# One core, a conditioned recurrent block with an MLP: the first stage put in a set order, with the stores of 1/rms, the sums of weights and the squares moved

## The chip, the cores and the metric

The kernel runs on one core of one Trainium2 chip. The metric is the device time of one execution in microseconds (us). Lower is better. TensorE (PE in the profile) does the matrix products; its weight loads have a row of their own (PEld). VectorE is DVE, ScalarE is ACT, GpSimd is POOL, and SyncE (SP) issues most of the DMAs.

## The reference

For B = 2 sequences of L = 2048 tokens with D = 512 channels, everything in float32:

```python
# _L0_cond_ref: a linear layer whose weight is scaled per sequence
styles = w @ (affine_w * gain).T + affine_b
ws = weight[None, :, :] * styles[:, None, :]
dcoefs = jax.lax.rsqrt(jnp.sum(ws * ws, axis=2) + 1e-08)
xm = x * styles[:, None, :]
y = jnp.einsum('blc,oc->blo', xm, weight)
y = jnp.clip(y * dcoefs[:, None, :] + bias, -CLAMP, CLAMP)

# _L0_attn_ref: a gated linear recurrence, then a gated MLP
h = _rms_norm(hidden_states, norm_w)
gate = jax.nn.gelu(h @ fc_gate_w.T + fc_gate_b, approximate=False)
hs = h @ fc_w.T + fc_b
r = jax.nn.sigmoid(h @ fc_r_w.T + fc_r_b)
i = jax.nn.sigmoid(h @ fc_i_w.T + fc_i_b)
a = jnp.exp(-8.0 * jax.nn.softplus(alpha) * r)
s = jnp.sqrt(1.0 - a * a) * hs * i          # o_t = a_t * o_(t-1) + s_t
hs2 = out * gate + residual
h2 = _rms_norm(hs2, norm2_w)
g2 = jax.nn.gelu(h2 @ mlp_gate_w.T + mlp_gate_b, approximate=False)
f2 = h2 @ mlp_fc_w.T + mlp_fc_b
return f2 * g2 @ out_w.T + out_b + hs2
```

Behind it stands a third part (several layer norms, a combining MLP and an int8 product), which the change doesn't touch.

## The kernel before

**Tiling.** The tokens are cut into NS = 4 blocks of S = 1024, two per sequence, with channels in the partitions. Every large product is a **unit**: the function `paired` computes a product of 2 x 2 blocks with seven products instead of eight, by sums of weights and sums of operands. A unit has seven steps. Each step multiplies one slot of the weight tile (slots 0 to 6; slots 4, 5, 2 and 6 hold the sums and differences) with one operand, for u = 0 and u = 1, four instructions each. Step 1 goes to the bank pair "a", whose values ScalarE copies out with the function `tap` (k1); steps 3 and 5 go on adding in the same banks and are copied again (k2, k3). Step 2 fills bank pair "b" and steps 4 and 7 pair "d". A product that adds to a bank must wait until the copy of the bank is taken. The argument `at` holds extra work: the functions under (n, u) are written right behind the half u of step n.

**Stages.** `cond(s)`, s = 0 to 3, is the first stage, one unit for each block (here: pass s). `recur(s, last)` is the recurrence, four units for each block. `up` is the first half of the MLP, six units for each block. `down` and what comes later are not touched.

**The start.** DMAs on SP bring `cols` (small vectors), `affT` (512 KB), `condT` (the first stage's weight, 1 MB) and `x` of the first block (2 MB). TensorE makes the styles (L326), then the sums of squares for dcoef: four row products into four groups of 32 columns (`rows_of`, L310), a copy on ScalarE (L311), and four transposing products (`columns_of`, L319). VectorE scales the weight by the styles (`style(0)`, L360) and makes its sums (L365 to L368), and makes the operand sums (`operand_sums`, L251 to L254). The first product of pass 0 comes behind all products of dcoef.

**1/rms.** `squares` adds up squares of the four outputs of a pass. `inv_rms` returns four functions: `total` (products with ones, L420), `log` and `exp` on ScalarE (L428, L432), and `step` on VectorE (L437 to L439) with four stores of 1 KB to `r_d` on SP's queue (L441). `then`, in the next pass or in the second unit of `up`, writes all four at once behind step 3. `normed_halves` loads a block again (L449), loads 1/rms broadcast to all partitions (L451), and multiplies the two in four chunks on VectorE (L454).

**Weights.** `load_rec(o, behind)` loads the weight of unit o of the recurrence in four DMAs and lets GpSimd make its sums (`combine`, L121 to L124). A copy of 1 x 8 values from `behind` into the tile (L537) keeps the DMAs from starting earlier than `behind` is written. `load_up(p)` does the same for the MLP, without such a copy. `load_rec(s, ...)` is called behind pass s with an operand sum of that pass as `behind`.

**The recurrence's rest.** `links` returns what is left of a unit after its products, and the next unit carries it out: `decay` and `rest_of_decay`, `scan` (VectorE, step 3), `gated` (step 4, which writes yr, L584 to L587), `square` of yr on ScalarE (L593, behind the first half of step 5) and `total`, an addition on VectorE (L597, behind step 5).

**Order.** A scheduler orders the instructions of every engine by priorities and by a simulated time. Inside `with ordered()` the engines TensorE, VectorE and ScalarE keep the order in which the program is written. Before, that holds for pass 3 and for the recurrence with the first unit of `up`. SP and GpSimd are always left to the scheduler.

Of the kernel before, what the change touches and what calls it, by code (L numbers as in the profile page):

```python
# [9 lines left out]
FP = mybir.dt.float32  # L10
BF = mybir.dt.bfloat16
AF = mybir.ActivationFunctionType
ALU = mybir.AluOpType
# [4 lines left out]
P = 128  # L18
# [32 lines left out]
def adaln_attn_ffn(ctx: ExitStack, tc: tile.TileContext, a: dict, out: bass.AP):  # L51
# [221 lines left out]
    def load_x(s):  # L273
# [3 lines left out]
        return t  # L277

    affT = row("affT").rearrange("p (j o) -> p j o", j=2)
# [3 lines left out]
    load_w(condT, a["condT"])  # L283
    x_first = load_x(0)
# [4 lines left out]
    nc.vector.tensor_copy(identb, ident)  # L289
    ones = const.tile([P, P], FP, name="ones")  # L290
    nc.vector.memset(ones, 1.0)
    one = ones[:, 0:1]
    epsc = const.tile([P, 1], FP, name="epsc")
    nc.vector.memset(epsc, 1e-6)

    groups = ident.rearrange("p (j r) -> p j r", r=G)
    summing = const.tile([P, G], FP, name="sums")
    nc.vector.tensor_reduce(summing, groups.rearrange("p j r -> p r j"), AX.X, ALU.add)  # L300
    apart = const.tile([P, 3, B], FP, name="apart")
    nc.vector.tensor_copy(apart, groups[:, 0:3, 0:B])
    nc.vector.tensor_add(apart[:, 0, :], groups[:, 0, 0:B], groups[:, 3, 0:B])

# [17 lines left out]

    ps = mm("ps_styles")
    for o in range(C):
        for j in range(2):
            nc.tensor.matmul(  # L326
                ps[:, o * B : o * B + B], affT[:, j, ts(o, P)], col("cond_512", j * B, B),
                start=(j == 0), stop=(j == 1),
            )
    for o in range(C):  # L330
        nc.vector.tensor_scalar(
            styles[:, o, :], ps[:, o * B : o * B + B], 1.0 / 16.0, col("L0_cond_affine_b", o),
            ALU.mult, ALU.add,
        )
# [3 lines left out]
    nc.vector.tensor_mul(st2[:, :, 0:B], styles, styles)  # L338
    wsq = []
    for c in range(C):  # L340
        t = tp.tile([P, T], FP, tag="k", name=f"wsq_{c}")
        nc.scalar.activation(t, condT[:, c, :], AF.Square)
        wsq.append(t)
    rows_k = tp.tile([P, T], FP, tag="k", name="ps_dcoef_k")
    rows_of("ps_dcoef", [(st2[:, c, :], wsq[c]) for c in range(C)], rows_k)
    ps = columns_of("ps_dcoef", rows_k, summing[:, 0:B])
    dflat = dcoef.rearrange("p c b -> p (c b)")
    dv = small.tile([P, 2, C * B], FP, name="dv")
    nc.vector.tensor_scalar(
        dv[:, 0, :], ps.rearrange("p c b -> p (c b)"), 1e-8, None, ALU.add  # L350
    )
    nc.scalar.activation(dflat, dv[:, 0, :], AF.Sqrt)
    nc.vector.reciprocal(dflat, dflat)
    refine(dflat, dv[:, 0, :], dv[:, 1, :])


    def style(b):
        w = w_cond[b]
        for c in range(C):
# [5 lines left out]
        nc.vector.tensor_add(w[:, 4], w[:, 2], w[:, 3])  # L365
        nc.vector.tensor_sub(w[:, 5], w[:, 4], w[:, 0])
        nc.vector.tensor_sub(w[:, 2], w[:, 0], w[:, 2])
        nc.vector.tensor_sub(w[:, 6], w[:, 1], w[:, 5])  # L368

    style(0)  # L370

# [4 lines left out]
    e_, u_, l_, d_, m_ = (sa[:, k, :] for k in range(5))  # L376
    nc.vector.tensor_scalar(m_, al, -1.0, None, ALU.mult)
    nc.vector.tensor_tensor(e_, al, m_, ALU.min)
    nc.scalar.activation(e_, e_, AF.Exp)
    nc.vector.tensor_scalar(u_, e_, 1.0, None, ALU.add)  # L380
    nc.scalar.activation(l_, u_, AF.Ln)
    nc.vector.tensor_scalar(d_, u_, -1.0, None, ALU.add)
    nc.vector.tensor_sub(d_, e_, d_)
    nc.vector.reciprocal(u_, u_)
    nc.vector.tensor_mul(d_, d_, u_)
    nc.vector.tensor_add(l_, l_, d_)
    nc.vector.tensor_scalar(m_, al, 0.0, None, ALU.max)
    nc.vector.tensor_add(l_, l_, m_)
    nc.vector.tensor_scalar(kal, l_, -8.0, None, ALU.mult)


    aw = col("aw", 0, 6)
    smx = small.tile([P, 2], FP, name="smx")
    nc.vector.reduce_max(smx[:, 0:1], aw, AX.X)
    nc.vector.tensor_scalar(wsm, aw, smx[:, 0:1], None, ALU.subtract)
    nc.scalar.activation(wsm, wsm, AF.Exp)
    nc.vector.reduce_sum(smx[:, 1:2], wsm, AX.X)
    nc.vector.reciprocal(smx[:, 1:2], smx[:, 1:2])
    nc.vector.tensor_scalar(wsm, wsm, smx[:, 1:2], None, ALU.mult)

# [8 lines left out]
    def inv_rms(tot, m, s):  # L409
# [25 lines left out]
        def step():  # L435
            r, q = held["r"], held["q"]
            nc.vector.scalar_tensor_tensor(q, held["ps"], D * 1e-6, q, ALU.add, ALU.mult)  # L437
            nc.vector.tensor_scalar(q, q, -0.5 / D, 1.5, ALU.mult, ALU.add)
            nc.vector.tensor_mul(r, r, q)  # L439
            for j in range(4):  # L440
                nc.sync.dma_start(r_d[m, s][:, ts(j, n)], r[32 * j : 32 * j + 1])  # L441

        return total, log, exp, step

# [16 lines left out]

    def then():
        while rest:
            for f in rest.pop(0):
                f()

# [9 lines left out]
    def cond(s):  # L476
        b = s // PER_S
        xs = operands(x_first if s == 0 else load_x(s), f"xT_{s}")
        y = {}

# [5 lines left out]
        def tap(u, ps, n):  # L486
            o = u if n < 3 else u + 2
            t = tp.tile([P, T], FP, tag="k", name=f"k{n}")
            nc.scalar.activation(
                t, ps, AF.Identity, scale=dcoef[:, o, b : b + 1], bias=col("L0_cond_bias", o)  # L490
            )
            return t
# [20 lines left out]

        at = {(3, 1): [then]}
        if s == NS - 1:

            Bt, chunks = rec_norm(0)
            ahead[:] = operand_sums(Bt, "hT_0")
            at[2, 1] = chunks[0:2]
            at[4, 1] = chunks[2:4]  # L520
            at[6, 1] = ahead[1][0:1]
        paired([w_cond[b]], xs, f"y_{s}", tap, put(0, a_), put(0, b_), out21, put(2, b_), at)
# [5 lines left out]
        rest.append(inv_rms(tot, 1, s))  # L528
        return xs

# [18 lines left out]
    chain = {}  # L549

    def merged(*ds):
        got = {}
        for d in ds:
            for k, fs in d.items():
                got.setdefault(k, []).extend(fs)
        return got

    def links(s, o, r, i, f, g, last, new, tots):
# [36 lines left out]
        def total():  # L595
# [8 lines left out]
            (1, 0): [decay], (1, 1): [rest_of_decay], (3, 1): [scan], (4, 1): [gated],  # L604
            (5, 0): [square], (5, 1): [total],
        }

    def recur(s, last):
        new = small.tile([P, C], FP, tag="carry", name=f"carry_{s}")
        tots = []  # L610
        for o in range(C):
# [27 lines left out]
            elif o == 1 and rest:  # L639
                total, log, exp, step = rest.pop(0)  # L640
                at = merged(at, {(3, 1): [total], (4, 1): [log], (5, 1): [exp], (6, 1): [step]})
            elif o >= 2:
                if o == 2:
                    Bt, chunks = rec_norm(s + 1) if s + 1 < NS else up_norm(0)
                    at = merged(at, {(2, 1): chunks[0:1], (6, 1): chunks[1:3]})
                else:
                    ahead[:] = operand_sums(Bt, f"hT_{s + 1}")
                    at = merged(at, {(2, 1): chunks[3:4], (6, 1): ahead[1][0:1]})
# [7 lines left out]

    def load_up(p):
        w = weight(f"w_up_{p}", {1: "A", 2: "B", 5: "C"}.get(p))
        for u in range(2):
            for k, n in ((0, "w_mg"), (2, "w_mf")):  # L660
# [9 lines left out]
    def up(s, xs, parts, at):  # L670
        for p in parts:
# [26 lines left out]
            def out22(u, ps, kept):  # L698
# [5 lines left out]
                [w_up[p]], xs, f"up_{s}_{p}", keep, out1(a_), out1(b_), out21, out22,  # L704
                at if p == 0 else {(3, 1): [then]} if p == 1 else {},
            )

    w_dn = []
# [9 lines left out]

    def ordered():
        return tc.manual_schedule(  # L720
            engines={mybir.EngineType.PE, mybir.EngineType.DVE, mybir.EngineType.Activation}
        )
# [898 lines left out]
```

## Time and profile before

| what | us |
|---|---|
| median of 3 runs (lowest, highest) | 2043.91 (2043.42, 2048.09) |
| the profiled execution | 2045.46 |
| its span, first to last instruction | 2043.7 |
| mean granted TensorE clock in it | 0.996 |
| first product of pass 0 (y_a) starts | 15.16 |
| first product of the recurrence (rec_a) starts | 120.75 |
| first product of the MLP (up_a) starts | 509.94 |

How much each engine works in the stages that the change edits, by the view of windows (us from the span's start; columns: length, then busy time and count of TensorE, its weight loads, VectorE, ScalarE and GpSimd, then TensorE's granted clock, the busy share of the DMA engines, and GB/s):

```profile
80.00:100.00 20.00, 19.34 (x46) 8.22 (x44) 18.74 (x18) 9.72 (x12) 14.04 (x8) 1.00 0.79 270
100.00:150.00 50.00, 45.62 (x109) 19.84 (x110) 31.31 (x33) 22.62 (x29) 12.19 (x9) 0.97 0.44 155
...
120.00:144.00 24.00, 24.00 (x58) 10.61 (x57) 11.76 (x13) 8.42 (x12) 5.93 (x4) 1.00 0.57 201
144.00:168.00 24.00, 24.00 (x64) 10.39 (x63) 12.67 (x15) 20.22 (x24) 0.00 (x0) 1.00 0.23 65
168.00:192.00 24.00, 24.00 (x58) 10.61 (x57) 16.93 (x17) 17.21 (x20) 0.00 (x0) 1.00 0.15 45
...
528.00:552.00 24.00, 21.37 (x53) 8.89 (x52) 9.98 (x13) 8.91 (x13) 0.00 (x0) 0.93 0.16 66
```

A stretch in which TensorE's busy time equals its length has no wait of TensorE in it. The granted clock is a mean over the stretch.

### The profile page before, as it was taken

Reading aid. Unit: us, or ns where it says so; the run is one execution under the profiler, and the core shown is the slowest. Engines: PE = TensorE matmul, PEld = TensorE weight load, DVE = VectorE, ACT = ScalarE, POOL = GpSimd, SP = SyncE. Lnnn points to the kernel's source line nnn. Section 1 sums busy time; section 2 is a strip of 40 time slices with the busy share of each in tenths; the row PEclk is TensorE's granted clock in tenths of the full one; section 3 lists DMA queues with packets and bytes.
Section 4 is the critical chain, followed back from the end, with each engine's and each line's share of the span. In section 5 each row is a group of like instructions: output and inputs, shape, how many; then the busy total and the mean of one; then the engine's idle time right before and its main releaser. Section 6 shows DMA issues by size and latency. Waiting matters only on the chain.

```text
span 2043.7 us, 17016 instructions
## 1 busy us (share of the span) xinstructions
PE 2016.0 (99%) x6374; PEld 1067.9 (52%) x6374; DVE 1195.5 (58%) x1798; ACT 653.2 (32%) x861; POOL 157.9 (8%) x126
## 2 busy tenths in 40 slices
PE   8999999999999999999999999999999999999997
PEld 4444444444444444444444444434877777777774
DVE  6766666667533324234325475476588678678675
ACT  4547777776422222222221000001302302302301
POOL 1420000012100000000010000072000000000000
PEclk9999999999999999999999999999999999999999
DMA  6731213232212212111335766624111111111000
GB/s 214 260 136 52 83 52 95 60 113 82 93 42 76 78 41 93 41 42 52 102 116 179 225 223 216 220 94 165 41 43 62 60 45 62 61 43 62 21 21 21
DMA packets 83971, 193.54 MB, mean 95 GB/s; under 512 B 6544, under 2 KB 34742, under 8 KB 79792
## 3 DMA queue, kind: packets, MB, share of 16 engines
q1 hardware_dynamic: 79280, 175.67, 25.3%
q0 software_dynamic: 4608, 16.78, 2.5%
q8 instruction: 50, 0.82, 0.2%
q14 instruction: 33, 0.27, 0.0%
HBM read 133.27 MB, written 58.75 MB: 94 GB/s over the span
## 4 chain that ended last, share of the span: by engine, by line
PE 93%; DVE 4%; DMA 1%; issue 1%; ACT 0%; SPq 0%; DVEq 0%; ACTq 0%
PE up_a L132 16%; PE ps_h_a L132 11%; PE rec_a L132 10%; PE up_d L132 8%; PE dn_a L132 7%; PE ps_h_d L132 6%; PE rec_d L132 5%; PE ps_o L1397 5%; PE up_b L132 4%; PE dn_d L132 4%; PE ps_h_b L132 3%; PE rec_b L132 3%; PE y_a L132 2%; PE dn_b L132 2%; PE ps_f L1421 1%; PE y_d L132 1%
## 5 line engine op out<-in xcount | busy, mean ns | idle before, releaser
L132 PE MATMUL up_a<-h,w_up 128*128 128x512 f32 x384 | 172.6, 592 | 0.0
L132 PE MATMUL dn_a<-op,w_dn 128*128 128x512 f32 x384 | 167.4, 594 | 0.0
L699 DVE SCALAR_TENSOR_TENSOR prod<-up_d,cols,k 128x512 f32<-128x512 f32 x48 | 36.0, 751 | 200.7 <-ACT k L265 200.7
L265 ACT COPY k<-up_a 128x512 f32<-128x512 f32 x144 | 84.2, 585 | 195.4 <-PE up_a L132 195.4
L679 ACT ACTIVATE gate<-gate,cols 128x512 f32<-128x512 f32 x96 | 68.8, 721 | 218.3 <-DVE gate L678 218.3
L132 PE MATMUL up_a<-h2T,w_up 128*128 128x512 f32 x288 | 129.5, 592 | 0.0
L132 PEld LDWEIGHTS up_a<-h,w_up 128*128 128x128 f32 x384 | 72.9, 190 | 91.9 <-issue 89.7
L132 PEld LDWEIGHTS dn_a<-op,w_dn 128*128 128x128 f32 x384 | 72.2, 190 | 88.8 <-issue 86.5
L132 PE MATMUL rec_a<-hT,w_rec 128*128 128x512 f32 x256 | 115.6, 593 | 1.1 <-ACT k L265 1.1
L132 PE MATMUL rec_a<-h,w_rec 128*128 128x512 f32 x256 | 115.1, 592 | 0.0
L1397 PE MATMUL ps_o<-int_w,h 128*128 128x512 f32 x224 | 103.6, 605 | 0.0
L132 PEld LDWEIGHTS up_a<-h2T,w_up 128*128 128x128 f32 x288 | 54.7, 190 | 68.9 <-issue 68.9
L132 PE MATMUL up_d<-h,w_up 128*128 128x512 f32 x192 | 87.5, 599 | 0.0
L132 PE MATMUL up_b<-h,w_up 128*128 128x512 f32 x192 | 86.3, 592 | 0.0
L132 PE MATMUL dn_d<-op,w_dn 128*128 128x512 f32 x192 | 84.2, 595 | 0.0
L132 PEld LDWEIGHTS rec_a<-hT,w_rec 128*128 128x128 f32 x256 | 48.5, 190 | 63.0 <-issue 60.3
L132 PEld LDWEIGHTS rec_a<-h,w_rec 128*128 128x128 f32 x256 | 48.6, 190 | 61.2 <-issue 61.2
L265 ACT COPY k<-rec_a 128x512 f32<-128x512 f32 x96 | 55.7, 580 | 70.2 <-PE rec_a L132 70.0
L678 DVE TENSOR_TENSOR gate<-up_b,k 128x512 f32<-128x512 f32 x48 | 32.9, 690 | 76.1 <-PE up_b L132 74.7
L132 PE MATMUL up_d<-h2T,w_up 128*128 128x512 f32 x144 | 65.2, 592 | 0.0
L1397 PEld LDWEIGHTS ps_o<-int_w,h 128*128 128x128 f32 x224 | 40.2, 189 | 46.5 <-issue 46.5
L132 PE MATMUL ps_h_a<-tT,w_int 128*128 128x256 f32 x256 | 64.2, 385 | 0.0
(389 smaller groups left out, 3475.4 us busy)
## 6 DMA issues: line engine op xcount, KB each, us to landing
pp_d<-prod SPq DMA_DIRECT2D x48, 512.0 KB
op<-pp_d SPq DMA_DIRECT2D x16, 1536.0 KB
x<-in_xT SPq DMA_DIRECT2D x4, 2048.0 KB
y_d<-y SPq DMA_DIRECT2D x16, 512.0 KB
h<-y_d SPq DMA_DIRECT2D x4, 2048.0 KB
yr<-y_d SPq DMA_DIRECT2D x16, 512.0 KB
hs_d<-yr SPq DMA_DIRECT2D x16, 512.0 KB
h<-hs_d SPq DMA_DIRECT2D x4, 2048.0 KB
```

What stands on the lines that cost most here:

```text
L132: ins = nc.tensor.matmul(ps, ws[k // 2][:, slot, k % 2, ts(u, P)], xs[k], start=(first and k == 0), stop=(last and k == n - 1), skip_group ...
L265: nc.scalar.copy(t, ps)
L678: nc.vector.tensor_add(gate[u][:, half], ps, kept)
L679: nc.scalar.activation(gate[u][:, half], gate[u][:, half], AF.Gelu, bias=col("L0_attn_mlp_gate_b", fs[u]),)
L699: nc.vector.scalar_tensor_tensor(prod[u][:, b_], ps, col("L0_attn_mlp_fc_b", fs[u]), kept, ALU.add, ALU.add)
L1397: nc.tensor.matmul(ps, h1[:, c, ts(j, P)], w2[:, c, :], start=(c == 0), stop=(c == C - 1))
L1421: nc.tensor.matmul(ps, qT[:, ts(c, P)], rq[:, c, :], start=(c == 0), stop=(c == C - 1))
```

## The change

1. **Pass 0 in a set order.** `with ordered()` now holds for passes 0 and 3. The preparations become functions that are called at chosen places: the constants, the styles, the scaling and the sums of the weight (`style` returns eight functions), the small work on alpha and aw (`alpha_1` to `alpha_4`), and the weight of the second sequence (`style(1)`) spread over steps 4 to 7. `condT` is loaded in two halves and the first x in four quarters. The rows of dcoef come between the two halves of step 1, its columns behind step 1, and the copies k1 are written behind them.
2. **Idle products.** `busy(n)` writes n products of ones with ones, 128 x 128, into a bank that nobody reads: 9 before the styles and 10 behind them.
3. **1/rms.** The four stores become a fifth function, `store`, on ScalarE's queue. `then` is gone: the five functions are spread over steps 4 to 7 of the next pass, and over steps 3 to 7 of a unit in the recurrence and in `up`.
4. **Pass 3.** The four chunks of the norm go behind steps 2 (two), 3 (one) and the first half of 5 (one), instead of two behind step 2 and two behind step 4.
5. **Weights.** `load_rec` is called for units 0, 1, none, and 2 and 3 behind the passes 0 to 3, and `behind` is the last output of the pass (y[1]). `load_up` has a `behind` too: the same output of pass 3 for w_up 0 to 2, and the last gate of the first unit of `up` for w_up 3 to 5.
6. **Squares of yr.** `square` moves from the first half of step 5 to behind step 6, `total` from behind step 5 to the first half of step 7.

```diff
+    for h in (0, 1):
+        nc.sync.dma_start(condT[:, 2 * h : 2 * h + 2, :], by_chunks(a["condT"])[:, 2 * h : 2 * h + 2, :])
+    x_first = halves("x_0")
+    for h, half in ((0, a_), (1, a_), (0, b_), (1, b_)):
+        of = slice(2 * h, 2 * h + 2)
+        nc.sync.dma_start(x_first[:, of, half], by_chunks(a["xT"][0])[:, of, half])
...
+    idle = mm("idle")
+    def busy(n):
+        for _ in range(n):
+            nc.tensor.matmul(idle[:, 0:P], ones, ones, start=True, stop=True)
...
+        def store():
+            r = held["r"]
             for j in range(4):
-                nc.sync.dma_start(r_d[m, s][:, ts(j, n)], r[32 * j : 32 * j + 1])
-        return total, log, exp, step
+                nc.scalar.dma_start(r_d[m, s][:, ts(j, n)], r[32 * j : 32 * j + 1])
+        return total, log, exp, step, store
...
-    def then():
-        while rest:
-            for f in rest.pop(0):
-                f()
+    def parts_of_rest(*keys):
+        if not rest:
+            return {}
+        return {k: [f] for k, f in zip(keys, rest.pop(0))}
+    AT = ((3, 1), (4, 1), (5, 1), (6, 1), (7, 1))
...
     def cond(s):
         b = s // PER_S
-        xs = operands(x_first if s == 0 else load_x(s), f"xT_{s}")
-        y = {}
+        at = parts_of_rest((4, 0), *AT[1:])
+        if s == 0:
+            busy(9)
+            constants()
+            styles_of()
+            busy(10)
+            parts = style(0)
+            for f in parts[0:2]:
+                f()
+            nc.vector.tensor_mul(st2[:, :, 0:B], styles, styles)
+            wsq = squares_of_weight()
+            for f in parts[2:6]:
+                f()
+            xs, sums = operand_sums(x_first, "xT_0")
+            sums[0]()
+            sums[1]()
+            other = style(1)
+            at = {
+                (2, 1): [sums[2], parts[7], sums[3], alpha_1], (3, 1): [alpha_2],
+                (4, 1): [alpha_3] + other[0:2], (5, 1): [alpha_4] + other[2:4],
+                (6, 1): other[4:6], (7, 1): other[6:8],
+            }
+        else:
+            xs = operands(load_x(s), f"xT_{s}")
+        y, late = {}, []
...
-            nc.scalar.activation(
+            late.append(lambda: nc.scalar.activation(
                 t, ps, AF.Identity, scale=dcoef[:, o, b : b + 1], bias=col("L0_cond_bias", o)
-            )
+            ))
+            if s == 0 and n == 1:
+                if u == 0:
+                    late.insert(0, dcoef_rows(wsq))
+                    return t
+                dcoef_columns(late.pop(0))
+                parts[6]()
+            while late:
+                late.pop(0)()
             return t
...
-        at = {(3, 1): [then]}
...
-            at[2, 1] = chunks[0:2]
-            at[4, 1] = chunks[2:4]
-            at[6, 1] = ahead[1][0:1]
+            at = merged(
+                at, {(2, 1): chunks[0:2], (3, 1): chunks[2:3], (5, 0): chunks[3:4], (6, 1): ahead[1][0:1]}
+            )
...
-            (5, 0): [square], (5, 1): [total],
+            (6, 1): [square], (7, 0): [total],
...
-                at = merged(at, {(3, 1): [total], (4, 1): [log], (5, 1): [exp], (6, 1): [step]})
+                at = merged(at, parts_of_rest(*AT))
...
+        nc.vector.tensor_copy(w[0:1, 0:4, 0, 0:2 * P:P], behind)
...
-                at if p == 0 else {(3, 1): [then]} if p == 1 else {},
+                at if p == 0 else parts_of_rest(*AT) if p == 1 else {},
...
-        with ordered() if s == NS - 1 else nullcontext():
-            xs = cond(s)
-        if s == 0:
-            style(1)
-        load_rec(s, xs(5)[0][0:1, 0:8].rearrange("p (a b) -> p a b", b=2))
+        with ordered() if s in (0, NS - 1) else nullcontext():
+            done = cond(s)
+        for o in ((0,), (1,), (), (2, 3))[s]:
+            load_rec(o, done)
     for p in range(3):
-        load_up(p)
+        load_up(p, done)
...
-        up(0, xs, (0,), merged(chain, {(2, 1): sums[2:4]}))
+        done = up(0, xs, (0,), merged(chain, {(2, 1): sums[2:4]}))
     for p in range(3, FC // 2):
-        load_up(p)
+        load_up(p, done)
```

More of the change, by code (lines that the diff above doesn't have):

```diff
@@ L277, in load_x, with ordered @@
         return t
+    def ordered():
+        return tc.manual_schedule(
+            engines={mybir.EngineType.PE, mybir.EngineType.DVE, mybir.EngineType.Activation}
+        )
     affT = row("affT").rearrange("p (j o) -> p j o", j=2)
@@ L282, in adaln_attn_ffn @@
     condT = part(weight("condT"), C, D)
-    load_w(condT, a["condT"])
-    x_first = load_x(0)
+    for h in (0, 1):
[4 more added lines that the diff above has]
+        nc.sync.dma_start(x_first[:, of, half], by_chunks(a["xT"][0])[:, of, half])
+    ones = const.tile([P, P], FP, name="ones")
+    nc.vector.memset(ones, 1.0)
+    one = ones[:, 0:1]
     ident = const.tile([P, P], FP, name="ident")
@@ L288, in adaln_attn_ffn, with constants @@
     identb = const.tile([P, P], BF, name="identb")
[L289 to L292, printed above, removed]
     epsc = const.tile([P, 1], FP, name="epsc")
-    nc.vector.memset(epsc, 1e-6)
-    groups = ident.rearrange("p (j r) -> p j r", r=G)
     summing = const.tile([P, G], FP, name="sums")
-    nc.vector.tensor_reduce(summing, groups.rearrange("p j r -> p r j"), AX.X, ALU.add)
     apart = const.tile([P, 3, B], FP, name="apart")
-    nc.vector.tensor_copy(apart, groups[:, 0:3, 0:B])
-    nc.vector.tensor_add(apart[:, 0, :], groups[:, 0, 0:B], groups[:, 3, 0:B])
+    def constants():
+        groups = ident.rearrange("p (j r) -> p j r", r=G)
+        nc.vector.memset(epsc, 1e-6)
+        nc.vector.tensor_copy(identb, ident)
+        nc.vector.tensor_reduce(summing, groups.rearrange("p j r -> p r j"), AX.X, ALU.add)
+        nc.vector.tensor_copy(apart, groups[:, 0:3, 0:B])
+        nc.vector.tensor_add(apart[:, 0, :], groups[:, 0, 0:B], groups[:, 3, 0:B])
     def rows_of(name, parts, t):
@@ L320, in columns_of @@
         return ps
[L323 to L328, printed above, removed]
-            )
[L330 to L333, printed above, removed]
-        )
+    idle = mm("idle")
@@ new lines, in busy, with styles_of @@
+    def busy(n):
+        for _ in range(n):
+            nc.tensor.matmul(idle[:, 0:P], ones, ones, start=True, stop=True)
+    def styles_of():
+        ps = mm("ps_styles")
+        for o in range(C):
+            for j in range(2):
+                nc.tensor.matmul(
+                    ps[:, o * B : o * B + B], affT[:, j, ts(o, P)], col("cond_512", j * B, B),
+                    start=(j == 0), stop=(j == 1),
+                )
+        for o in range(C):
+            nc.vector.tensor_scalar(
+                styles[:, o, :], ps[:, o * B : o * B + B], 1.0 / 16.0, col("L0_cond_affine_b", o),
+                ALU.mult, ALU.add,
+            )
@@ L336, in adaln_attn_ffn @@
     st2 = tp.tile([P, T], FP, tag="k", name="st2")[:, : C * G].rearrange("p (c g) -> p c g", g=G)
     nc.gpsimd.memset(st2, 0.0)
[L338 to L345, printed above, removed]
@@ L346, in adaln_attn_ffn, with squares_of_weight @@
-    ps = columns_of("ps_dcoef", rows_k, summing[:, 0:B])
+    def squares_of_weight():
+        wsq = []
+        for c in range(C):
+            t = tp.tile([P, T], FP, tag="k", name=f"wsq_{c}")
+            nc.scalar.activation(t, condT[:, c, :], AF.Square)
+            wsq.append(t)
+        return wsq
     dflat = dcoef.rearrange("p c b -> p (c b)")
     dv = small.tile([P, 2, C * B], FP, name="dv")
-    nc.vector.tensor_scalar(
-        dv[:, 0, :], ps.rearrange("p c b -> p (c b)"), 1e-8, None, ALU.add
-    )
@@ L352, in adaln_attn_ffn, with dcoef_rows, dcoef_columns @@
-    nc.scalar.activation(dflat, dv[:, 0, :], AF.Sqrt)
-    nc.vector.reciprocal(dflat, dflat)
-    refine(dflat, dv[:, 0, :], dv[:, 1, :])
+    def dcoef_rows(wsq):
+        t = tp.tile([P, T], FP, tag="k", name="ps_dcoef_k")
+        rows_of("ps_dcoef", [(st2[:, c, :], wsq[c]) for c in range(C)], t)
+        return t
+    def dcoef_columns(t):
+        ps = columns_of("ps_dcoef", t, summing[:, 0:B])
+        nc.vector.tensor_scalar(
+            dv[:, 0, :], ps.rearrange("p c b -> p (c b)"), 1e-8, None, ALU.add
+        )
+        nc.scalar.activation(dflat, dv[:, 0, :], AF.Sqrt)
+        nc.vector.reciprocal(dflat, dflat)
+        refine(dflat, dv[:, 0, :], dv[:, 1, :])
@@ L357, in style, with scale @@
     def style(b):
         w = w_cond[b]
-        for c in range(C):
+        def scale(c):
             nc.vector.tensor_scalar(
@@ L364, in style @@
             )
[L365 to L370, printed above, removed]
+        return [lambda c=c: scale(c) for c in range(C)] + [
+            lambda: nc.vector.tensor_add(w[:, 4], w[:, 2], w[:, 3]),
+            lambda: nc.vector.tensor_sub(w[:, 5], w[:, 4], w[:, 0]),
+            lambda: nc.vector.tensor_sub(w[:, 2], w[:, 0], w[:, 2]),
+            lambda: nc.vector.tensor_sub(w[:, 6], w[:, 1], w[:, 5]),
+        ]
     al = col("L0_attn_alpha", 0, C)
@@ L376, in adaln_attn_ffn, with alpha_1, alpha_2, alpha_3 @@
     e_, u_, l_, d_, m_ = (sa[:, k, :] for k in range(5))
[L377 to L389, printed above, removed]
     aw = col("aw", 0, 6)
     smx = small.tile([P, 2], FP, name="smx")
[L394 to L399, printed above, removed]
+    def alpha_1():
+        nc.vector.tensor_scalar(m_, al, -1.0, None, ALU.mult)
+        nc.vector.tensor_tensor(e_, al, m_, ALU.min)
+        nc.vector.reduce_max(smx[:, 0:1], aw, AX.X)
+        nc.vector.tensor_scalar(wsm, aw, smx[:, 0:1], None, ALU.subtract)
+    def alpha_2():
+        nc.scalar.activation(e_, e_, AF.Exp)
+        nc.scalar.activation(wsm, wsm, AF.Exp)
+    def alpha_3():
+        nc.vector.tensor_scalar(u_, e_, 1.0, None, ALU.add)
+        nc.scalar.activation(l_, u_, AF.Ln)
+        nc.vector.tensor_scalar(d_, u_, -1.0, None, ALU.add)
+        nc.vector.tensor_sub(d_, e_, d_)
+        nc.vector.reduce_sum(smx[:, 1:2], wsm, AX.X)
+        nc.vector.reciprocal(smx[:, 1:2], smx[:, 1:2])
+        nc.vector.tensor_scalar(wsm, wsm, smx[:, 1:2], None, ALU.mult)
+    def alpha_4():
+        nc.vector.reciprocal(u_, u_)
+        nc.vector.tensor_mul(d_, d_, u_)
+        nc.vector.tensor_add(l_, l_, d_)
+        nc.vector.tensor_scalar(m_, al, 0.0, None, ALU.max)
+        nc.vector.tensor_add(l_, l_, m_)
+        nc.vector.tensor_scalar(kal, l_, -8.0, None, ALU.mult)
     def squares(tot, y):
@@ L460, in adaln_attn_ffn, with merged @@
     rest = []
-    def then():
-        while rest:
-            for f in rest.pop(0):
-                f()
+    def parts_of_rest(*keys):
[3 more added lines that the diff above has]
+    AT = ((3, 1), (4, 1), (5, 1), (6, 1), (7, 1))
+    def merged(*ds):
+        got = {}
+        for d in ds:
+            for k, fs in d.items():
+                got.setdefault(k, []).extend(fs)
+        return got
     def rec_norm(s):
@@ L488, in tap @@
             t = tp.tile([P, T], FP, tag="k", name=f"k{n}")
-            nc.scalar.activation(
+            late.append(lambda: nc.scalar.activation(
                 t, ps, AF.Identity, scale=dcoef[:, o, b : b + 1], bias=col("L0_cond_bias", o)
-            )
+            ))
+            if s == 0 and n == 1:
+                if u == 0:
+                    late.insert(0, dcoef_rows(wsq))
+                    return t
+                dcoef_columns(late.pop(0))
+                parts[6]()
+            while late:
+                late.pop(0)()
             return t
@@ L518, in cond @@
             ahead[:] = operand_sums(Bt, "hT_0")
-            at[2, 1] = chunks[0:2]
-            at[4, 1] = chunks[2:4]
-            at[6, 1] = ahead[1][0:1]
+            at = merged(
+                at, {(2, 1): chunks[0:2], (3, 1): chunks[2:3], (5, 0): chunks[3:4], (6, 1): ahead[1][0:1]}
+            )
         paired([w_cond[b]], xs, f"y_{s}", tap, put(0, a_), put(0, b_), out21, put(2, b_), at)
@@ L528, in cond @@
         rest.append(inv_rms(tot, 1, s))
-        return xs
+        return y[1][0:1, 0:8].rearrange("p (a b) -> p a b", b=2)
     w_rec = []
@@ L549, in adaln_attn_ffn @@
     chain = {}
[L551 to L556, printed above, removed]
     def links(s, o, r, i, f, g, last, new, tots):
@@ L639, in recur @@
             elif o == 1 and rest:
-                total, log, exp, step = rest.pop(0)
-                at = merged(at, {(3, 1): [total], (4, 1): [log], (5, 1): [exp], (6, 1): [step]})
+                at = merged(at, parts_of_rest(*AT))
             elif o >= 2:
@@ L655, in adaln_attn_ffn, with load_up @@
     w_up = [None] * (FC // 2)
-    def load_up(p):
+    def load_up(p, behind):
         w = weight(f"w_up_{p}", {1: "A", 2: "B", 5: "C"}.get(p))
+        nc.vector.tensor_copy(w[0:1, 0:4, 0, 0:2 * P:P], behind)
         for u in range(2):
@@ L704, in up @@
                 [w_up[p]], xs, f"up_{s}_{p}", keep, out1(a_), out1(b_), out21, out22,
-                at if p == 0 else {(3, 1): [then]} if p == 1 else {},
+                at if p == 0 else parts_of_rest(*AT) if p == 1 else {},
             )
+        return gate[1][0:1, 0:8].rearrange("p (a b) -> p a b", b=2)
     w_dn = []
@@ L717, in load_dn @@
         w_dn.append(w)
[L719 to L722, printed above, removed]
     for s in range(NS):
-        with ordered() if s == NS - 1 else nullcontext():
-            xs = cond(s)
-        if s == 0:
-            style(1)
-        load_rec(s, xs(5)[0][0:1, 0:8].rearrange("p (a b) -> p a b", b=2))
+        with ordered() if s in (0, NS - 1) else nullcontext():
+            done = cond(s)
+        for o in ((0,), (1,), (), (2, 3))[s]:
+            load_rec(o, done)
     for p in range(3):
-        load_up(p)
+        load_up(p, done)
     carry = None
```

## The prediction

> **What bounds the kernel now.** I read the page's busy times first, then TensorE's own timeline, then TensorE's list of waits, and last all engines around each wait. The busy row says what kind of time is left to win.
>
> ```profile
> PE 2016.0 (99%) x6374; PEld 1067.9 (52%) x6374; DVE 1195.5 (58%) x1798; ACT 653.2 (32%) x861; POOL 157.9 (8%) x126
> ```
>
> TensorE bounds nearly all of the span, and the change removes no product of the computation. So only TensorE's idle time (2043.7 - 2016.0 = 27.7 us) and its slowed time can go. The start of its timeline:
>
> ```profile
> 5.03 3.54 PE L326 MATMUL ps_styles<-cols,affT 128*128 128x2 f32 x16 [5.03 <-DMA affT<-in_affT]
> 10.10 3.48 PE L310 MATMUL ps_dcoef_r<-wsq,st 128*32 128x512 f32 x8 [1.52 <-DVE sa L385]
> 14.24 1.05 PE L319 MATMUL ps_dcoef_c<-sums,ps_dcoef_k 128*128 128x2 f32 x8 [0.67 <-ACT ps_dcoef_k L311]
> 15.16 3.68 PE L132 MATMUL y_a<-x,w_cond 128*128 128x512 f32 x8
> ```
>
> The columns are start, duration, instruction, count, and in brackets the idle time before it with what ended it. The first useful big product starts at 15.16, behind the styles and the whole chain of dcoef. From there a step (8 instructions) takes 3.43 and a unit of seven steps 24.0, wherever no wait is listed. The list of waits:
>
> ```profile
> PE ps_styles L326 <- DMA affT<-in_affT: 5.0, 1, 5.0
> PE ps_f L1421 <- DVE pw L1487: 4.6, 3, 3.4
> PE y_d L132 <- DVE y L500: 3.1, 1, 3.1
> PE up_a L132 <- ACT k L265: 2.6, 1, 2.6
> PE rms_ps L420 <- DVE sq L406: 1.9, 1, 1.9
> PE rec_a L132 <- ACT k L265: 1.1, 2, 0.7
> ```
>
> The 4.6 us at ps_f are at the kernel's end, which the change leaves alone. The others lie where it edits. Pass 3 of the first stage:
>
> ```profile
> 111.47 2.24 POOL L124 TENSOR_TENSOR w_rec<-w_rec 128x512 f32<-128x512 f32 x1
> 114.72 1.40 DVE L500 SCALAR_TENSOR_TENSOR y<-y_d,dcoef,k 128x512 f32<-128x512 f32 x2
> 115.51 1.96 PE L132 MATMUL y_d<-x,w_cond 128*128 128x512 f32 x3 [3.12 <-DVE y L500]
> ```
>
> VectorE reads the bank (L500) late: two norm chunks just ahead of it held it for 4.49 us, while GpSimd summed w_rec. The second place is the end of the recurrence:
>
> ```profile
> 528.78 1.22 DVE L586 TENSOR_TENSOR yr<-yr,g 128x1024 f32<-128x1024 f32 x1
> 530.03 1.06 ACT L593 ACTIVATE sq<-yr 128x1024 f32<-128x1024 f32 x1 [3.86 <-DVE yr L586]
> 531.00 0.57 ACT L265 COPY k<-up_a 128x512 f32<-128x512 f32 x1
> 531.62 2.50 PE L132 MATMUL up_a<-hT,w_up 128*128 128x512 f32 x4 [2.63 <-ACT k L265]
> ```
>
> ScalarE stands 3.86 us at the square of yr. The copy that TensorE needs (L265) is queued behind it.
>
> **Part 1, gaps after the first product.** Each is the start of a row less the start of the row before and its own 3.43 (or 1.72 for four instructions).
> - The total of pass 2 at 101.25, against 95.74 + 3.43: 2.08, of which 0.10 for changing the product's shape stays; 1.98 goes. In the new order this total comes after the first half of step 4, 1.72 later. The sums of w_up and w_rec that slowed the adds of squares (2.31 instead of 1.22 at 98.88) are no longer there, so the rest of the wait is covered too.
> - y_d at 115.51, against 108.79 + 3.43: 3.29. The chunks move to step 2, step 3 and behind the first half of step 5; no w_rec sum runs there. The first chunk waited 2.40 for the broadcast of 1/rms, which landed behind a 2 MB load and w_rec's 1 MB; the latter is gone.
> - The eight products after it take 5.24 (115.51 to 120.75) instead of 3.43: 1.81 for a halved clock.
> - Copies of k waited for in the recurrence: 479.73 against 477.45 + 1.72, 0.56; 504.69 against 502.15 + 1.72, 0.82; 531.62 against 527.11 + 1.72, 2.79. The square moves from step 5 to step 6, behind the copies of k and out21. What is late next is ScalarE's gate sigmoid and VectorE's add at step 7; neither is needed before step 2 of the next unit, over 3 us away.
> - Slow products after the last: 2.29 - 1.72 and (533.91 to 538.57) 4.66 - 3.43: 1.80.
>
> Sum: 1.98 + 3.29 + 1.81 + 0.56 + 0.82 + 2.79 + 1.80 = 13.05.
>
> The rows show half speed after idle times of 3.12 and 2.63 us. The Trainium skill ("TensorE: Matmul & The Clock Gate", Part 1) says that the clock falls only after an idle window of about 3.4 us; by it neither gap would have cost clock and the sum would be 3.6 smaller, but the measurement decides.
>
> **Part 2, the start.** Three things must be there for the first product. TensorE: an f32 product is two instructions (8 products are x16 above), so busy(9) is 18. At the 3.54/16 = 0.22 of the styles' row that is 4.0 from about 1.0 (ones is set at 0.83 for 0.17), ending at 5.0, when affT lands: no delay. Sixteen styles instructions take 3.5 at that pace, or 16 x 0.13 = 2.1 at the dcoef_c row's pace (1.05/8) if the idle products have raised the clock; busy(10) is 20 x 0.13 = 2.6, or 4.4 if not. So TensorE is free between 9.7 (all raised) and 12.9 (nothing raised). VectorE: four styles 0.60 and two scalings 0.88 after the products, 8.6 to 10.1. DMA: the DMA view of the first 20 us shows some 400 GB/s, so half of condT and a quarter of x behind 0.58 MB are there at about 9 to 10. I take 10.6, between TensorE's bounds and nearer the raised clock, because a window of mostly busy time raised it in this trace (from 0.22 per weight load at 5 us to 0.13 at 14 us).
>
> The dcoef products are still on TensorE, now between the halves of step 1 and after it. Eight row products at full clock take 1.07 elsewhere (ps_sh_r at 1133.39); dcoef_c takes 0.92 to the next start; two changes of shape 0.1 each: 2.1. So 15.16 - 10.6 - 2.1 = 2.46 is won. Then the dcoef chain (0.17, 0.21, 0.19, three of 0.16, in all some 1.5 with handovers) and two k copies of 0.78 must fit in step 2, 3.43 long; VectorE has to finish t2 first, which needs the last quarter of x (13.4 to 15 at 300 to 400 GB/s). The room is about 0.5, and I put 0.5 against it (bounds 0 and 2).
>
> **Part 3, moves costed at nothing.** Thirty-two stores of 1/rms (eight times four) go from SP's queue to ScalarE's. No row shows ScalarE issuing one. SP's four take 1.13 (80.59), the slowest single issue in the rows is 1.09 (idx_m), so four cost between 0 and 4.4. They stand at the end of step 7; the next copy of k is due when step 3 starts, 6.87 - 1.72 = 5.15 after it can begin, which hides them even at 4.4. Sums of weights: w_rec 2, 3 and w_up 0 to 2 (20 GpSimd adds of 1.27 alone) all come after pass 3, and w_up 3 to 5 after the first up unit. Each gets a 1x8 VectorE copy first; behind the five copies stand only the last operations of pass 3, which finish earlier. Twenty DMAs of about 0.5 on SP and 5 MB at 400 GB/s end near 127; w_rec 2 is needed 48 us after the recurrence starts, about 159. VectorE is the one that can suffer:
>
> ```profile
> 80.48 1.22 DVE L251 TENSOR_TENSOR xT<-x 128x1024 f32<-128x1024 f32 x1
> ...
> 85.93 2.30 DVE L254 TENSOR_TENSOR xT<-x,xT 128x1024 f32<-128x1024 f32 x1
> ```
>
> The same operation beside a GpSimd add takes 1.08 more. Twenty times that is 21.6, and VectorE is idle for 12.2 and 11.3 us in the first two 24 us stretches of the recurrence (busy 11.76 and 12.67): covered, barely. Without that cover it would be 0 to 5 us. The Trainium skill ("SBUF — State Buffer", Who interferes with whom) speaks against crowding them: a GpSimd instruction that reads SBUF excludes a VectorE one with two SBUF inputs for its whole length. By that each add could hold VectorE 1.27, in all 25 us, 2 more than the room.
>
> **Sum.** 13.05 + 2.46 - 0.5 = 15.0. The profiled execution took 2045.46 (span 2043.7 and 1.8 around it), which gives 2030.5; it lies 1.5 above the median of the runs, 2043.91, from which I predict 2028.9.
>
> **Rivals.**
> (a) The start wins nothing, 0.14: the clock stays low until 13 or the quarters land late, so the first product starts at 12.9 and step 3 waits 2. Against it stands the room of 0.5 only. 13.05 + 0.16 - 2 = 11.2 won: 2032.7.
> (b) A new wait in the recurrence, 0.16: the crowded GpSimd adds put VectorE behind in units 2 and 3, ScalarE's square waits, TensorE stalls 2 to 5 and pays 1.8 in clock. For it: exactly this happened at 528. Against: the square now has 3 us more. 15.0 - 3.8 to 6.8: 2033 to 2036.
> (c) Slower, 0.06: ScalarE's queue. If four stores hold it so long that the copy of k comes late, TensorE stalls eight times, each with some 1.8 of clock. To eat 15.0 and 6.1 more, each must cost 2.6, so the hold must pass 5.15 + 0.8 = 6.0, or 1.5 per store. At 2 per store (8.0) the loss is 8 x (2.85 + 1.8) = 37: 2066. Against: the slowest issue in the rows is 1.09.
> (d) The order doesn't take effect or other waits replace all of it, 0.06: 2043 or thereabouts.
>
> **Numbers.** The forecast has 0.58 with its own range 2026 to 2031.5 (start 1.2 earlier, medians 1.5 apart, against 2 at step 3). The range for 8 in 10 adds (a) and most of (b): 2025.8 to 2035.5. About 0.3% (6.1 us) is what a measurement here can tell from no change: faster means below 2037.8. Forecast, (a) and (b) all lie there, 0.88; same 0.06; slower 0.06.
>
> **What would show it.** Right: y_a starts near 10.6; no wait of TensorE between there and the end of the first up unit longer than 0.5; rec_a starts near 111 instead of 120.75; full clock at both old places; GpSimd's adds of w_up after 113. Wrong: TensorE waiting for k in step 3 of pass 0 or in the first three units of the recurrence; ScalarE's idle times ahead of a copy of k ended by VectorE's product of 1/rms; a low clock after 14 us.

## The result, and the profile after

| what | before | after |
|---|---|---|
| median of 22 runs each (lowest, highest), us | 2043.91 (2041.12, 2048.09) | 2041.66 (2036.49, 2045.28) |
| ratio of after to before, 95% interval | | 0.9979 [0.9973, 0.9986] |
| the profiled execution, us (its span) | 2045.46 (2043.7) | 2037.24 (2035.5) |
| first product of pass 0, us | 15.16 | 10.66 |
| first product of the recurrence, us | 120.75 | 116.93 |
| first product of the MLP, us | 509.94 | 504.53 |

By the ratio the change gained 0.2%, some 4 us (the medians differ by 2.3), where 15 were forecast and a range of 2025.8 to 2035.5 was given. The forecast was wrong. The page's busy row and TensorE's list of waits after the change (us in total, times, longest):

```profile
PE 2016.1 (99%) x6404; PEld 1073.6 (53%) x6412; DVE 1188.6 (58%) x1804; ACT 652.4 (32%) x861; POOL 155.1 (8%) x126
```

```profile
PE y_a L132 <- ACT k L562: 5.1, 2, 2.7
PE ps_f L1491 <- DVE pw L1557: 3.9, 2, 3.4
PE up_a L132 <- ACT k L265: 1.3, 1, 1.3
PE idle L340 <- DVE ones L298: 1.1, 1, 1.1
```

Every wait that the forecast meant to remove is gone: y_d behind VectorE, the total of squares, and the copies k at the recurrence's end. Two lines are new, and both name a copy k on ScalarE. TensorE's timeline shows where they are; the start of the kernel first:

```profile
1.05 3.67 PE L340 MATMUL idle<-ones 128*128 128x128 f32 x18 [1.05 <-DVE ones L298]
5.02 1.92 PE L346 MATMUL ps_styles<-cols,affT 128*128 128x2 f32 x16 [0.30 <-DMA affT<-in_affT]
6.80 4.07 PE L340 MATMUL idle<-ones 128*128 128x128 f32 x20
10.66 1.97 PE L132 MATMUL y_a<-x,w_cond 128*128 128x512 f32 x4
```

That is the predicted start (10.6). Now all engines in pass 1, from step 6 on:

```profile
56.26 1.48 DVE L476 TENSOR_TENSOR rms<-rms 128x256 f32<-128x256 f32 x1
57.42 1.44 POOL L123 TENSOR_TENSOR w_rec<-w_rec 128x512 f32<-128x512 f32 x1
...
57.77 0.71 ACTq L481 DMA_DIRECT2D r_d<-rms  x2
...
58.52 0.78 ACT L562 ACTIVATE k<-y_a,cols,dcoef 128x512 f32<-128x512 f32 x1 [4.46 <-DVE y L582]
58.55 0.51 ACTq L481 DMA_DIRECT2D r_d<-rms  x2
...
59.35 1.13 PE L132 MATMUL y_a<-xT,w_cond 128*128 128x512 f32 x2 [2.67 <-ACT k L562]
```

ACTq is ScalarE's own queue issuing a DMA. The stores of 1/rms (L481) are written behind step 7. In the queue two of them stand in front of the second copy k3, at the end of step 5. They need VectorE's last product of 1/rms (L476), which takes 1.48 instead of the 0.43 it had at 80.14 before, because GpSimd sums w_rec beside it. So ScalarE does no arithmetic for 4.46, of which the two stores' own issue is the last 0.71; the copy is late, and TensorE waits for it. The second unit of `up` shows the same, with three stores in front of the copy:

```profile
545.12 1.37 DVE L476 TENSOR_TENSOR rms<-rms 128x256 f32<-128x256 f32 x1
...
546.52 0.79 ACTq L481 DMA_DIRECT2D r_d<-rms  x3
...
547.35 0.58 ACT L265 COPY k<-up_a 128x512 f32<-128x512 f32 x1 [3.68 <-DMA r_d<-rms]
```

Three waits of this kind cost 59.35 - 54.80 - 1.72 = 2.83 in pass 1, 86.88 - 82.54 - 1.72 = 2.62 in pass 2, and 547.99 - 543.06 - 3.43 = 1.50 in `up`: 6.95. The forecast for the profiled execution was 2030.5; with these 6.95 it would have been 2037.45, and 2037.24 was measured. That the two agree so closely is partly luck: the forecast also set 0.5 against the last quarter of x, which wasn't paid. What these three places have in common is that they lie outside `ordered()`. In pass 3 and in the recurrence, where the order is kept, the stores stand behind step 7 and TensorE has no such wait.

### The profile page after: what moved, and what is told of

Read it like the earlier page. It is cut to its first block, busy times and chain, and to the rows that moved or that the text cites. A ratio compares the mean times of both kernels' runs of the same rounds, so it can differ in the third digit from the quotient of the medians.

```text
span 2035.5 us, 17108 instructions
## 1 busy us (share of the span) xinstructions
PE 2016.1 (99%) x6404; PEld 1073.6 (53%) x6412; DVE 1188.6 (58%) x1804; ACT 652.4 (32%) x861; POOL 155.1 (8%) x126
## 4 chain that ended last, share of the span: by engine, by line
PE 96%; DVE 2%; DMA 1%; ACT 1%; issue 0%; ACTq 0%; SPq 0%; DVEq 0%
PE up_a L132 16%; PE ps_h_a L132 11%; PE rec_a L132 11%; PE up_d L132 8%; PE dn_a L132 7%; PE ps_h_d L132 6%; PE rec_d L132 5%; PE ps_o L1467 5%; PE up_b L132 4%; PE dn_d L132 4%; PE ps_h_b L132 3%; PE rec_b L132 3%; PE y_a L132 2%; PE dn_b L132 2%; PE ps_f L1491 1%; PE y_d L132 1%
```

## The experiments

Twelve more runs were made. Each was timed together with the kernel before, whose median moved between 2045.17 and 2046.3, so ratios are compared, with their 95% intervals. The theory: the stores on ScalarE's queue, put between the two copies k3 by the scheduler, make TensorE wait (A). Rivals: VectorE's lateness beside GpSimd does it by itself (B); the table loads of Ln and Exp do it (C).

**The stores back on SP's queue.**

```diff
-                nc.scalar.dma_start(r_d[m, s][:, ts(j, n)], r[32 * j : 32 * j + 1])
+                nc.sync.dma_start(r_d[m, s][:, ts(j, n)], r[32 * j : 32 * j + 1])
```

> The changed kernel with one edit: the stores of 1/rms are on SP's queue again; the order of TensorE's and VectorE's instructions stays the same, instruction for instruction. Theory A (ScalarE stands at the store, put by the scheduler between the two copies k3 in the passes 1 and 2 and in the second unit of up, and TensorE waits for the second copy): the waits at 56, 84 and 546 us (2.83, 2.62 and 1.49, with restarts 7.2 in all) go, the profiled execution comes to about 2030, the median to about 2029 to 2030.5, and the runs lie closer together than the changed kernel's 2036.5 to 2045. Rival B (VectorE is late because GpSimd sums w_rec beside it, and the store is only named by the list of waits): the waits stay, 2037 to 2042. Rival C (the tables loaded for Ln and Exp in steps 4 and 5 make the copy late): the waits stay, 2037 to 2042.

Measured: 2032.98 (2032.64 to 2033.8) against 2045.17, ratio 0.9937 [0.9923, 0.9950]. In pass 1, from all engines:

```profile
57.14 3.17 PE L132 MATMUL y_a<-xT,w_cond 128*128 128x512 f32 x7
57.34 0.78 ACT L562 ACTIVATE k<-y_a,cols,dcoef 128x512 f32<-128x512 f32 x1 [0.94 <-PE y_a L132]
...
58.59 1.48 DVE L476 TENSOR_TENSOR rms<-rms 128x256 f32<-128x256 f32 x1
```

VectorE's product takes the same 1.48 and now comes after the copy, and TensorE runs through. All three waits are gone and the runs lie within 1.2 us of each other. B and C fall: both would have kept the waits. The time is above what was expected: the profiled execution took 2032.64 where about 2030 was expected, and the median is 2.5 above the end of its range. In this execution the first product came at 13.09 instead of 10.66, which is 2.4 of it (see the start below).

**The set order everywhere, the stores left on ScalarE.**

```diff
-        with ordered() if s in (0, NS - 1) else nullcontext():
+        with ordered():
             done = cond(s)
...
-    up(0, xs, range(1, FC // 2), {})
+    with ordered():
+        up(0, xs, (1,), {})
+    up(0, xs, range(2, FC // 2), {})
```

> The changed kernel with the set order on all four passes and on the second unit of up; the stores stay on ScalarE's queue, behind step 7, where they are written. Theory A: the three waits go as in the run with SP's stores, 2029 to 2031; nothing else is lost as long as VectorE makes the operand sums of the next pass in time for step 3. Rival B: VectorE stays late, so ScalarE waits at step 7 instead and the next copy k1 has 5 us of room: TensorE's waits go too, but the product of 1/rms still takes 1.3 to 1.5 us in VectorE's rows. Rival C: the waits stay, 2037 to 2042.

> The kernel with all four passes and the second unit of up in a set order, once more, as the base of the three others of this call: 2030 to 2033, first product of pass 0 between 10.6 and 13.1 us in the profile, no wait of TensorE over 1 us before the end of up.

> The all-ordered kernel as the base of this call: 2030 to 2033.

Measured three times: 2031.89, 2031.48 and 2032.88; ratios 0.9930 [0.9916, 0.9944], 0.9934 [0.9920, 0.9948], 0.9933 [0.9919, 0.9947]. So the stores may stay on ScalarE if their place is kept. What A expected is shown from this side too. (B expected the same here; the SP run is the one that separates them.) Two waits of 0.7 and 0.5 remain at step 3 of the passes 2 and 3, where the stores and four squares stand ahead of the copies k1.

**Are GpSimd's sums needed for the wait?**

```diff
-        for o in ((0,), (1,), (), (2, 3))[s]:
+        for o in ((), (0,), (1,), (2, 3))[s]:
             load_rec(o, done)
```

> The changed kernel with load_rec called for units none, 0, 1, and 2 and 3 behind the passes 0 to 3, so that GpSimd makes no sums in pass 1; the stores stay on ScalarE's queue in the scheduler's place. If GpSimd's sums are needed for the wait, beside the store's place, pass 1 has no wait of TensorE (or under 1 us) and pass 2 keeps its 2.6. If the store's place alone makes the wait, pass 1 keeps 2 us or more. Time 2034 to 2042.

Measured: 2041.33 (2038.78 to 2043.58), ratio 0.9978 [0.9968, 0.9989]. Pass 1, now without sums on GpSimd:

```profile
55.28 0.42 DVE L476 TENSOR_TENSOR rms<-rms 128x256 f32<-128x256 f32 x1
...
55.73 0.71 ACTq L481 DMA_DIRECT2D r_d<-rms  x2
...
57.32 1.98 PE L132 MATMUL y_a<-xT,w_cond 128*128 128x512 f32 x4 [0.54 <-ACT k L562]
```

The product of 1/rms takes 0.42 and the wait shrinks from 2.67 to 0.54. Pass 2, with the sums, waits 4.45 where 2.6 was expected, and the clock halves behind it. The changed kernel itself, in the next section, has 4.54 there in another execution, so this edit is not needed for the longer wait. Two waits at y_d, 1.4 in sum, are new. So the wait has two parts: the place of the stores, without which there is none (the SP run), and VectorE's lateness beside GpSimd, which sets most of its length.

**The changed kernel again.**

> The changed kernel once more. The waits at about 56, 84 and 546 us are there in every execution, since they come from the order of ScalarE's queue; whether the clock falls behind them depends on where the clock's window of 3.41 us lies. If so, the times spread over 2036 to 2045 again and a profile shows none, one or more stretches at half clock behind those waits, each worth up to 1.8 (3.4 where it lasts two windows).

Measured: 2039.77 (2035.73 to 2045.57, 10 runs), ratio 0.9966 [0.9953, 0.9978]. Its profiled execution took 2042.8. The same stretch behind the wait of pass 1, by windows, first from the earlier execution, then from this one (length; busy time and count of TensorE, weight loads, VectorE, ScalarE, GpSimd; granted clock; DMA share; GB/s):

```profile
59.35:62.90 3.55, 3.55 (x9) 1.64 (x10) 3.55 (x5) 2.14 (x3) 1.72 (x1) 1.00 0.13 53
```

```profile
59.71:63.19 3.48, 3.48 (x4) 1.51 (x5) 2.26 (x3) 0.61 (x1) 1.71 (x1) 0.51 0.11 47
```

The wait before both is 2.67. In one execution nine products follow at full clock, in the other four at half. But the clock is only a part of the 5.56 between the two executions. Their rows give 0.36 for the start, 1.66 and 1.39 for the clock behind the waits of the passes 1 and 2, and 2.08 because the wait of pass 2 is longer:

```profile
90.98 3.37 PE L132 MATMUL y_a<-xT,w_cond 128*128 128x512 f32 x4 [4.54 <-ACT k L562]
```

It was 2.46 in the earlier execution. Ahead of 1/rms, VectorE's operand sums ran more slowly beside GpSimd this time, one of them (L252) in 2.28 instead of 1.21. So the waits are there in both executions, as expected, but not with the same length.

Over all 32 runs of the changed kernel the mean granted clock goes with the time: the 14 runs at 0.997 or 0.998 took 2035.73 to 2040.34, the 9 at 0.996 took 2037.45 to 2043.65, and the 9 at 0.994 or 0.995 took 2040.67 to 2045.57. Stretches at half clock and the longer wait are thus the likely reason why its runs spread over 10 us, and why its first profile, which shows no stretch at half clock behind the three waits, lies 4.4 below its median. Only these two executions were traced, so the parts of the 4.4 are argued, not measured. The kernels without these waits keep within 1.2 to 4.4, with five or six runs each.

**The square of yr, alone and taken back.** First the kernel before with this part of the change only, then the all-ordered kernel without it:

```diff
-            (5, 0): [square], (5, 1): [total],
+            (6, 1): [square], (7, 0): [total],
```

> The kernel before with one part of the change alone: the square of yr behind step 6 and its addition in step 7. If the square's place ahead of the copy k3 made the waits at the recurrence's end, they go without the later sums of weights as well: 4 to 6 us faster than the kernel before. If VectorE's lateness beside GpSimd's sums makes TensorE wait by another way, 0 to 3 us faster.

> The all-ordered kernel with the square of yr back behind the first half of step 5 and its addition behind step 5. If the square's place alone made the waits at the recurrence's end (0.56, 0.82 and 2.79, and 1.80 for the clock), they come back: 5 to 6 us slower than the base. If GpSimd's sums of w_up, now made later, had made yr late, the square's move is worth little by itself: 0 to 1.5 slower, and ScalarE's wait for yr before the square at the end of the recurrence is under 2 us instead of 3.86.

Measured: alone, 2040.19 (2038.72 to 2045.1) against 2046.14, ratio 0.9978 [0.9969, 0.9988], 4.5 us by the ratio; TensorE's list has no wait for a copy of k any more. Taken back, 2032.28, ratio 0.9937 [0.9924, 0.9951], not told apart from its base (0.9934). ScalarE's waits for yr in front of the square, first in the kernel before with the square moved (460 to 560 us), then in the all-ordered kernel with it back (the whole span):

```profile
ACT sq L593 <- DVE yr L586: 2.2, 1, 2.2
```

```profile
ACT sq L667 <- DVE yr L660: 1.7, 2, 1.5
```

In the kernel before there were three such waits from 460 to 560 us, 7.4 in all, the longest 3.86. With the square behind the copies, TensorE doesn't wait for a copy behind it even where yr is 2.2 late. With the square back and the rest of the change in place, yr is hardly late; that the later sums of w_up are the part that does this is likely, but they weren't moved alone. Each of the two takes away these waits (a wait of 0.3 remains in the second), so one is worth little on top of the other.

**The weights as in the kernel before,** on the all-ordered kernel:

```diff
-        return y[1][0:1, 0:8].rearrange("p (a b) -> p a b", b=2)
+        return xs(5)[0][0:1, 0:8].rearrange("p (a b) -> p a b", b=2)
...
-        for o in ((0,), (1,), (), (2, 3))[s]:
-            load_rec(o, done)
+        load_rec(s, done)
...
-        nc.vector.tensor_copy(w[0:1, 0:4, 0, 0:2 * P:P], behind)
```

(The last edit is in `load_up` only.)

> The all-ordered kernel with the weights loaded as in the kernel before: load_rec(s) behind pass s with the pass's operand sum as the mark, load_up without a mark. If the crowding of GpSimd's sums into pass 2 and 3 and the recurrence's end is what made VectorE late there, waits of TensorE come back at pass 3 (1 to 5 us) and perhaps in the last units of the recurrence: 2 to 7 us slower than the base. If the new places of chunks, total and square are enough, within 1 us of the base.

Measured: 2037.27 (2036.35 to 2038.09), ratio 0.9960 [0.9946, 0.9973], 5.8 above its base's median. The wait was expected at y_d of pass 3 and comes at its step 3:

```profile
92.12 1.19 ACTq L481 DMA_DIRECT2D r_d<-rms  x4
...
93.36 3.90 ACT L441 ACTIVATE sq<-y 128x1024 f32<-128x1024 f32 x4 [8.29 <-DMA r_d<-rms]
...
97.98 2.93 PE L132 MATMUL y_a<-xT,w_cond 128*128 128x512 f32 x3 [3.50 <-ACT k L562]
```

Here the stores are in their written place. ScalarE still stands there for 8.29, because VectorE, beside GpSimd's sums of w_up, comes late to 1/rms; four squares and two copies k1 are queued behind. Behind the wait the clock is low: the eight products take 6.49 (97.98 to 104.47) instead of 3.43. The wait and the clock, 3.50 and 3.06, are about the loss of 5.8.

**The idle products.** The all-ordered kernel without them, then with two instead of ten behind the styles:

```diff
...
-            busy(9)
             constants()
             styles_of()
-            busy(10)
```

> The all-ordered kernel without the 19 idle products. If they raise the clock for the real ones, the first product starts earlier (9.5 to 10.2, when the styles are scaled and the first quarter of x has landed), but 3.4 to 6.8 us of products run at half speed: 1 to 3 us slower than the base. If they only hold the first product back, 0 to 1.5 us faster.

```diff
-            busy(10)
+            busy(2)
```

> The all-ordered kernel with 2 idle products behind the styles instead of 10. If the ten hold the first product back, it starts at 9.5 to 10 (the first quarter of x lands at 9.5) in every execution, and the median is 0 to 1.5 us below the all-ordered kernel's 2031.5 to 2031.9. If fewer idle products leave the clock low at the start, the first products run at half speed: 0 to 2 us above.

Measured: 2032.97, ratio 0.9940 [0.9926, 0.9954], and 2033.2, ratio 0.9936 [0.9925, 0.9948]. The first median is 1.5 above that of the base beside it (2031.48), but the intervals overlap. The second had no base beside it; its ratio is 0.0002 to 0.0006 above the base's three, 0.4 to 1.2 us, which the intervals don't tell apart. TensorE's first products of pass 0, without idle products and with two:

```profile
9.55 3.53 PE L132 MATMUL y_a<-x,w_cond 128*128 128x512 f32 x4 [1.09 <-DVE w_cond L385]
```

```profile
9.57 3.75 PE L132 MATMUL y_a<-x,w_cond 128*128 128x512 f32 x4 [2.16 <-DMA x<-in_xT]
```

Both start an us earlier than the changed kernel's 10.66 and take 3.5 to 3.8 for four instructions instead of 1.97. In three of the ten profiles with both sets of idle products these won nothing: the styles took 3.54 and the second set 4.5 to 4.6, which is the slow pace (1.92 and 2.5 where it is fast), and the first product came at 12.86 to 13.09. What the idle products win in clock they mostly lose again by holding the first product back; their worth, if any, is about 1.5 us and not settled.

**The set order with the stores on SP.**

> The all-ordered kernel with the stores on SP's queue. The all-ordered kernel still has two waits of TensorE at step 3 of the passes 2 and 3 (0.70 and 0.5) in which ScalarE has stood behind the stores and the squares. If the stores' wait for VectorE is their cause, they go, and the median is 1 to 1.5 below the all-ordered kernel of the same call. If the four squares ahead of the copies are enough to make them, the time is within 0.5 of it.

Measured: 2031.37 (2029.79 to 2032.84), ratio 0.9924 [0.9909, 0.9938], beside 2032.88 for the all-ordered kernel timed with it. The two small waits at step 3 are gone from its list. The medians differ by the 1.5 that was expected, but the intervals overlap. This version, and the all-ordered one, beat both kernels clearly.

## Why the prediction was wrong

- **The gaps after the first product (13.05).** Right. All five places are free of waits in the profile after. The all-ordered kernel, which has all parts of the change and none of the new long waits, is 13.3 to 14.3 below the kernel before by the medians of its three measurements, with waits of 0.7 and 0.5 left; 15.0 was forecast.
- **The start (2.46 won, the first product at 10.6).** Right in the profile (10.66). But it varies with the clock: 9.54 to 13.09 in the ten profiles with both sets of idle products, within or close to the bounds 9.7 and 12.9 that were given. The 0.5 set against the last quarter of x wasn't paid: step 3 of pass 0 starts without a listed wait.
- **The stores on ScalarE's queue, costed at nothing.** This step failed. It said: "They stand at the end of step 7; the next copy of k is due when step 3 starts, 6.87 - 1.72 = 5.15 after it can begin, which hides them even at 4.4." Two things in it were wrong. The place is that of the program only where the order is kept. The passes 1 and 2 and the second unit of `up` are left to the scheduler, which put two stores between the copies k3 of a pass, where the room is one half step, 1.72, and three in front of both copies in `up`. And the price isn't the issue: two stores took 0.50 to 0.71 on ScalarE's queue. It is ScalarE's wait for VectorE's 1/rms, most of the 4.46 in pass 1. The text had asked what is queued behind a waiting instruction for the square and not for the stores, though its last paragraph names this very sign of being wrong, an idle ScalarE ahead of a copy of k that ends with VectorE's product of 1/rms.
- **Rival (c)** named the right queue with the wrong price (1.5 for each store) and so gave it 0.06. The same mechanism at three places, with its wait instead of its issue, takes 6.95; the kernel is still faster, as forecast.
- **GpSimd's sums.** The crowded sums in the recurrence's first units did no harm: no wait of TensorE stands there, as the room of 12.2 and 11.3 said. What was missed is that the sums of w_rec 0 and 1 now fall on the very steps in which VectorE makes 1/rms (1.36 and 1.48 instead of 0.29 and 0.43 in pass 1), which sets most of the length of the new waits.
- **The clock.** The forecast paid 3.6 for the clock at the two old gaps, as the profile showed it. The kernel before was traced once, so whether it always pays at these two isn't known. The changed kernel pays at its new waits in one traced execution and not in the other, and with a longer wait in pass 2 this is the likely source of the 4.4 between the profile after and its median.

## What to carry to other kernels

A DMA issued from a compute engine's queue is an instruction of that engine: ask what it waits for, not only what its issue costs, and who is queued behind it. Where a scheduler orders the queue, the place in the program is no evidence of the place in the queue; find out for each block whether the order is kept before a cost is set to nothing. Two edits that remove the same wait are worth it once.

## What the runs showed of the hardware

TensorE's clock fell behind a wait of 2.67 in one execution and stayed full behind the same wait in another, so the length of a wait doesn't decide alone. The traces record when the clock changes. In each of the fourteen, these times lie whole multiples of 3.413 us apart, and the stretches at half clock ahead of the kernel's end last 3.41 (behind the waits of the changed kernel run again) or 6.83 (behind the 4.45 and the 3.50 above). If the time of each trace is cut at such steps, then behind the first 12 us the clock fell after every full-speed step in which TensorE's rows leave it idle for 2.08 or more (21 falls), and after none with 1.94 or less. The wait of 2.67 left 1.94 of idle time in one step in the earlier execution (55.20 to 58.61) and 2.64 in the other (56.27 to 59.68). So how a wait lies across the steps fits all that was seen; this was read from the traces afterwards, and no run was made to try it.

The Trainium skill ("TensorE: Matmul & The Clock Gate", Part 1) calls the window 3.4 us long and free-running, which agrees with these steps. Its rule that only a gap over about 3.4 us costs clock does not agree with the wait of 2.67.

A busy TensorE doesn't hold the clock by itself. After the change, by windows (columns as above), the styles' products of two columns and then the second set of idle products:

```profile
5.00:7.00 2.00, 1.98 (x18) 2.00 (x19) 0.02 (x1) 0.66 (x2) 0.00 (x0) 1.00 1.04 389
6.80:10.60 3.80, 3.80 (x22) 3.80 (x22) 3.55 (x11) 1.83 (x4) 0.00 (x0) 0.58 1.00 358
```

TensorE counts as busy for 1.98 of 2.00, nearly all of it with the narrow products, and right afterwards the clock is at 0.58 for the idle ones. Why was not tried; it fits that products of two columns don't count as activity, but no run here shows it.
